# Tasks in the attention loops of layers 2 and 3: columns beside the scores, norms and rotary turns in single steps, key pieces traced behind the slot products

## The chip, the cores and the metric

The kernel runs on one core of a Trainium2 chip. A core has a matrix engine (TensorE, PE in profiles; its weight loads are shown apart as PEld), a vector engine (DVE), a scalar engine (ACT), a general engine (POOL) and a queue engine (SP) that issues most transfers. Each engine takes its instructions in one fixed order and waits where one isn't ready. The metric is the time of one execution on the device in microseconds (us); the median over several runs counts.

## The reference, cut to what matters

A model of four layers; each adds a cross attention to the tokens x (16 batches of 112 tokens, 256 wide, 1792 tokens in all) and then a feed-forward part. The change lies in the attentions of layers 2 and 3 and in what follows them:

```python
# layer 2 attention: 16 heads of 16, keys and values from a context of 375 rows
q = (query @ Wq.T + bq).reshape(B, Sq, H, Dh)
q = q * cq + _rotate_half(q) * sq_          # keys are turned likewise
scores = jnp.einsum('bqhd,bkhd->bhqk', q, k) * scale
probs = jax.nn.softmax(scores, axis=-1)
ctx = jnp.einsum('bhqk,bkhd->bqhd', probs, v).reshape(B, Sq, H * Dh)
return ctx @ Wo.T + bo
# layer 2 feed-forward: norm, 8 experts, the best 2 of each token
xn = x * jax.lax.rsqrt(jnp.mean(x * x, axis=-1, keepdims=True) + eps) * ln_w
logits = xn @ Wg + bg
vals, idx = jax.lax.top_k(logits, K)
...
# the stack
x = x + jnp.tanh(g_xattn[2]) * _L2_xattn_ref(_layernorm(x, axis=-1), ctx_1024, ...)
x = x + jnp.tanh(g_ffn[2]) * _L2_ffn_ref(_layernorm(x, axis=-1), ...)
```

Layer 3 is the same in kind: no rotary turn, a mask on the scores, 9 experts.

## The kernel before

**The attention loop** (`attention16`) serves layers 2 and 3. Its unit is four heads of one batch, 64 units in all, and step s of 70 begins unit s and carries earlier ones on. In order, TensorE does in step s:

- `scores(s)`: queries against keys, four heads into the four banks of one PSUM tile `sc` (tag sS, one buffer), columns 0 to 374 of each bank. In the first six steps idle matmuls (`spins`) follow into columns 376 to 503 of the same banks. DVE then takes each row's least score: in layer 2 by one reduction over all four banks (line 854), in layer 3 by four passes, one a bank (line 858).
- the tasks of the table `between[s]` (below);
- `by_keys`, `values`, `by_keys`: scores once more with the keys on the partitions (tile `st`, three banks, tag sT, one buffer), exponentials on ACT out of it, and weights times values into the tile `mi`;
- transposes in `mi` (`by_queries`, `maxima`, `by_rows`), with small DVE and ACT work after each.

Then DVE does the tasks of `behind[s]`, and SP gets the loads of keys and values for a later batch. Scores, tasks and transposes are pinned: `keep_in_program_order` puts an instruction behind everything traced before it on its engine. What is not pinned is ordered by a planner, which takes at each point the earliest traced of what it holds to be ready. The program's own dependency tracking adds the waits between engines.

**Tasks** are work that lies beside the attention. Early in the loop: statistics of late token tiles (`moments_at`, `roots_at`), their scaled rows (`scaled_at`), transposes of those rows into `hT` (`rows_at`: PE, then an ACT copy), and the query groups 2 and 3 of layer 2 (1 to 3 of layer 3), four batches each. Later in the loop, from `Outcome.tasks`: for each pair of token tiles the output projection and its addition to x (`add`), the norm of the result in nine small pieces in `behind`, the transposes of the rows, and the router's logits (`route`). A task's PSUM space is `three()`, a tile of tag sT, which is the one buffer that `by_keys` uses too (a2bt and a3bt in the profile; st is a2st and a3st).

**Layer 2's queries** are turned (`rotary`, lines 595 to 602): four DVE instructions on 448 columns for each half of a group, eight in one go, and then eight stores into slots (`to_slots`).

**After layer 2's loop** (`Outcome.rest`, `chosen`, `softmax_of`, `dispatch`): the last pair of tiles is finished, the best two experts of each token are found on DVE, two matmuls count them (`cp`, `tp`), more DVE work follows, and 56 matmuls (`slot`, line 1112) give the slots of the tokens, which the gather of the experts' rows needs (`tok`). Into this chain `fill(n)` traces pieces of the keys and values of layer 3 for ten batches (40 pieces; k3b in the profile): 4, 4 and 8 in `rest`, 8 at the start of `dispatch`, the other 16 ahead of the slot matmuls. Layer 3 has no such pieces, and its chain has idle matmuls (`spin`) instead.

Of the kernel before, what the change touches and what calls it, by code (L numbers as in the profile page):

```python
# [86 lines left out]
def flamingo_kernel(ctx, tc, a, out):  # L87
# [159 lines left out]
    def norm_rows(n, bank, tr=None, act=True, scale_by=None, keep=None, h=None):  # L247

        pin = tc.keep_in_program_order if tr else free
        if h is None:  # L250
            h = scaled(n, pin, keep)
        tp = bank(f"tp{n}")
        for c in range(2):
            (tr or nc.tensor.transpose)(tp[:, c * P:(c + 1) * P], h[:, c * P:(c + 1) * P], ident)
        if scale_by is not None:
            for c in range(2):
                nc.scalar.activation(
                    hT[:, c, n * P:(n + 1) * P], tp[:, c * P:(c + 1) * P], AF.Identity,
                    scale=col(scale_by, c),
                )  # L260
            return
        dst, src = hT[:, :, n * P:(n + 1) * P], tp[:, :D].rearrange("p (c t) -> p c t", c=2)
        pin(nc.scalar.copy(dst, src) if act else nc.vector.tensor_copy(dst, src))
# [330 lines left out]

    def rotary(pool, tag, dst, src, cos, sin, sign, fixed=False):

        rot = pool.tile(list(src.shape), F32, tag="rot", name=f"rot{tag}", bufs=1)
        pin = tc.keep_in_program_order if fixed else lambda i: i
        pin(nc.vector.stream_shuffle(rot, src, half_on))
        pin(nc.vector.scalar_tensor_tensor(rot, rot, sign, sin, ALU.mult, ALU.mult))  # L600
        pin(nc.vector.scalar_tensor_tensor(dst, src, sign, cos, ALU.mult, ALU.mult))
        pin(nc.vector.tensor_tensor(dst, dst, rot, ALU.add))

# [102 lines left out]

    def query_group(pool, tag, qT, wq, q_out, G, ps=None, mm=None):
# [33 lines left out]
    class Outcome:  # L741
# [30 lines left out]
        def tasks(self, between, behind, bias):  # L772


            for n, at, slots in zip(
                    range(0, NT - 2, 2), (18, 27, 36, 45, 54, 63),
                    ((29, 30, 32), (38, 39, 41), (47, 48, 50), (56, 57, 59), (65, 66, 68),
                     (67, 68, 69))):
                between.setdefault(at, []).append(
                    lambda three, mm, tr, n=n: self.add(n, three(), mm, pinned))  # L780
                todo = [bias[n // 2], moments_at(n, 1), moments_at(n + 1, 1)]
                todo += [lambda n=n, i=i: self.part(n, i, pinned) for i in range(4)]
                todo += [lambda n=n + i: self.scale(n, pinned) for i in range(2)]
                for i, t in enumerate(todo):

                    s = at + 1 + i if at < 63 else 64 + i // 3
                    behind.setdefault(s, []).append(t)
# [11 lines left out]
        def rest(self, tag, bias):  # L799
            n = NT - 2  # L800
            self.add(n, ps_pair(f"{tag}ops"))
            bias[n // 2]()
            fill(4)
# [5 lines left out]
            fill(4)  # L809
            self.route(n, ps_o(f"{tag}r"))  # L810
            fill(8)

    def attention16(pool, pp, tag, qT, kTs, vs_, store, nm=None, maskT=None, tasks=({}, {}), spins=(0, 0)):
# [202 lines left out]
    def dispatch(pool, keep, tag, one, two, gates, n_e):  # L1016
# [9 lines left out]
        sel2 = sel.rearrange("p e n -> p (e n)")  # L1026
        fill(8)
        what = small([P, 2, 2 * NT], "what")
# [75 lines left out]
        for k in range(2):  # L1104
# [3 lines left out]
            )  # L1108
        fill(len(filler))
        ps = ps_mm(f"{tag}slot")  # L1110
        for i in range(2 * NT):
# [3 lines left out]
            )  # L1115
        spin(ps_o(f"{tag}spin2")[:, :P], 14, at_lo[:, 0, :])

# [405 lines left out]
    with tc.tile_pool(name="l1x", bufs=2) as pool, tc.tile_pool(  # L1523
# [22 lines left out]
        def key_rotations(pool):  # L1546
# [14 lines left out]
            def turn(b, c):  # L1561
                k = held[b, c]
                rotary(pool, f"k{b}_{c}", k, k, tabs[:, 0, :], tabs[:, 1, :], 1.0, True)
                nc.gpsimd.dma_start(kr_store[b, :, c, :], k)
# [80 lines left out]
    def q_out2(qc, ps, G):  # L1645
        for c in range(2):
# [4 lines left out]
            con[:, at:at + S].unsqueeze(1).to_broadcast([P, 4, S]) for at in (C_COS, C_SIN)  # L1651
        )
        for c in range(2):
            four = qc[:, c, :].rearrange("p (b t) -> p b t", b=4)
            rotary(q_at, f"q{G}_{c}", four, four, cos, sin, -1.0)

# [189 lines left out]
    with tc.tile_pool(name="l3x", bufs=2) as pool:  # L1846
# [16 lines left out]
        def group3(G):  # L1863
            return lambda three, mm, tr: queries3(G, three(), mm)

# [208 lines left out]
```

## Time and profile before

| | us |
|---|---|
| median of 3 runs | 3017.82 (3011.21 to 3028.72) |
| the profiled execution | 3033.68 |
| its span, first to last instruction | 3031.8 |
| layer 2's loop, from the first scores to the last projection | 1440.85 to 1758.7 |
| from there to the first expert matmul of layer 2 | 1758.7 to 1864.0 |
| layer 3's loop | 2297.09 to 2658.0 |
| from there to the first expert matmul of layer 3 | 2658.0 to 2702.3 |

The profile is one execution. Lines of its page and answers name the engine, the line of the code, the operation and the tiles as out<-in. In lists in order of time the first two numbers are start and length in us, and a bracket gives the idle time before the instruction and what ended it. In lists of waits the numbers are us in total, times, and the longest. In tables of stretches each engine's busy time is followed by its count of instructions, and the last three numbers are the granted clock of TensorE as a share of full speed, the share of busy transfers, and GB/s.

### The profile page before, as it was taken

To read this page: it belongs to the slowest core of one execution; us is meant where nothing else is said; L and a number is where in the kernel's file an instruction comes from. 1 tells how busy PE (TensorE), PEld (TensorE's weight loads), DVE (VectorE), ACT (ScalarE), POOL (GpSimd) and SP (SyncE) were. 2 spreads that over 40 slices of the span, in tenths; PEclk is the share of its full clock that TensorE was granted. 3 is DMA by queue.
4 is the path that set the end of the run, shared out by engine and by line. 5 is a ranking of instruction groups with operands and counts; after the bars stand their busy time and mean duration, and the time that the engine had idled before them with its cause. 6 is when DMAs were issued, how large, how long until landed. Compare 5 with 4: busy or idle time off the path is not lost. (4 is left out here: it accounts for less than half of the span.)

```text
span 3031.8 us, 50238 instructions
## 1 busy us (share of the span) xinstructions
PE 2811.4 (93%) x19789; PEld 1985.1 (65%) x19789; DVE 1579.5 (52%) x4642; ACT 1040.5 (34%) x2392; POOL 249.5 (8%) x260
## 2 busy tenths in 40 slices
PE   6998999999999999998798878999998899889997
PEld 4666876566666666655565556888885555567775
DVE  5677874466666666666556632232224565542221
ACT  3556973244444444522234422111112333301111
POOL 1000000100000000000000001222210000012321
PEclk9999999999999999999789979999999999989999
DMA  4011334412112111010122146565532222135553
GB/s 166 27 32 59 108 118 157 165 56 65 58 54 65 61 32 34 25 39 12 40 68 84 53 136 236 150 181 176 165 96 79 71 73 68 38 114 153 157 153 96
DMA packets 118866, 281.99 MB, mean 93 GB/s; under 512 B 26904, under 2 KB 86664, under 8 KB 109712
## 3 DMA queue, kind: packets, MB, share of 16 engines
q1 hardware_dynamic: 95920, 242.50, 23.9%
q0 software_dynamic: 19040, 31.83, 5.1%
q10 hardware_dynamic: 3664, 4.37, 0.5%
q8 instruction: 160, 2.62, 0.4%
q14 instruction: 82, 0.67, 0.1%
HBM read 214.92 MB, written 81.35 MB: 98 GB/s over the span
## 5 line engine op out<-in xcount | busy, mean ns | idle before, releaser
L272 PE MATMUL b3ab<-b3xT,w 128*128 128x256 f32 (+1 forms) x864 | 196.1, 385 | 0.5 <-DVE b3xT L1167 0.5
L272 PEld LDWEIGHTS b3ab<-b3xT,w 128*128 128x128 f32 (+1 forms) x864 | 155.0, 183 | 39.4 <-issue 11.6
L1183 ACT ACTIVATE b2gs<-b2ab,bias 128x256 f32<-128x256 f32 x144 | 68.2, 474 | 321.0 <-PE b2ab L272 280.2
L394 PE MATMUL a1vps<-w_l1v,a1cb 128*125 128x512 f32 x360 | 172.1, 602 | 0.9
L1184 DVE SCALAR_TENSOR_TENSOR b2hid<-b2ab,bias,b2gs 128x256 f32<-128x256 f32 x144 | 69.6, 483 | 194.9 <-ACT b2gs L1183 194.9
L394 PE MATMUL a1kps<-a1cb,w_l1k 128*128 128x375 f32 x480 | 165.2, 486 | 0.0
L486 ACT ACTIVATE a1pe<-a1pe,a1mx 112x375 f32<-112x375 f32 x256 | 153.3, 603 | 0.0
L272 PE MATMUL b2ab<-b2xT,wa 128*128 128x256 f32 x576 | 150.3, 384 | 0.6 <-DVE b2xT L1169 0.6
L272 PE MATMUL b2ab<-b2xT,wb 128*128 128x256 f32 x576 | 149.0, 381 | 0.0
L476 DVE CUSTOM_DVE_ANT_0 a1pe<-a1sc,nm 112x375 f32<-112x375 f32 x256 | 126.0, 544 | 43.9 <-PE a1sc L394 43.9
L397 PEld LDWEIGHTS a1tp<-ident,a1pe 112*125 112x125 f32 x768 | 98.4, 188 | 58.2 <-issue 41.3
L1189 DVE TENSOR_TENSOR b3hid<-b3ab,b3gs 128x256 f32<-128x256 f32 x108 | 45.7, 423 | 172.7 <-ACT b3gs L1188 172.7
L1194 PE MATMUL b2yo<-wc,b2hid 128*128 128x256 f32 x576 | 132.1, 382 | 2.9 <-DVE b2y L1199 0.6
L858 DVE CUSTOM_DVE_ANT_0 a3ms<-a3sc,first_cb 112x375 f32<-112x375 f32 x256 | 124.5, 543 | 17.3 <-PE a3sc L835 16.8
L1188 ACT ACTIVATE b3gs<-b3ab 128x256 f32<-128x256 f32 x108 | 41.3, 382 | 260.1 <-PE b3ab L272 233.5
L885 ACT ACTIVATE a3pT<-a3st 125x1008 f32<-125x1008 f32 x86 | 86.3, 1004 | 128.4 <-PE a3st L835 128.4
L1194 PEld LDWEIGHTS b2yo<-wc,b2hid 128*128 128x128 f32 x576 | 108.0, 190 | 21.3 <-DVE b2y L1199 7.0
L272 PEld LDWEIGHTS b2ab<-b2xT,wa 128*128 128x128 f32 x576 | 110.5, 192 | 16.4 <-DVE b2xT L1169 1.2
L272 PEld LDWEIGHTS b2ab<-b2xT,wb 128*128 128x128 f32 x576 | 110.6, 192 | 15.4
L854 DVE TENSOR_REDUCE a2mx<-a2sc 112x4 f32<-112x1500 f32 x64 | 109.6, 1713 | 18.4 <-PE a2sc L835 18.1
L394 PEld LDWEIGHTS a1kps<-a1cb,w_l1k 128*128 128x128 f32 x480 | 85.8, 190 | 49.1 <-DVE a1pT L400 3.3
L885 ACT ACTIVATE a2pT<-a2st 125x1008 f32<-125x1008 f32 x86 | 86.3, 1004 | 81.9 <-PE a2st L835 81.9
(481 smaller groups left out, 5648.9 us busy)
## 6 DMA issues: line engine op xcount, KB each, us to landing
w<-all_w SPq DMA_DIRECT2D x36, 704.0 KB
wa<-in_w_l2e1a SPq DMA_DIRECT2D x18, 1024.0 KB
wb<-in_w_l2e1b SPq DMA_DIRECT2D x18, 1024.0 KB
wc<-in_w_l2e SPq DMA_DIRECT2D x18, 1024.0 KB
all_w<-in_w SPq DMA_DIRECT2D x24, 704.0 KB
a2vs<-k2v SPq DMA_DIRECT2D x16, 750.0 KB
a2v<-a2vs SPq DMA_DIRECT2D x16, 750.0 KB
a3v<-a3vs SPq DMA_DIRECT2D x16, 750.0 KB
```

Source lines behind the costliest of these rows:

```text
L272: (mm or nc.tensor.matmul)(dst, lhs(k), rhs(k), start=(k == 0), stop=(k == 1))
L394: pin(nc.tensor.matmul(*args, **kw))
L397: pin(nc.tensor.transpose(*args))
L476: pin(nc.vector.tensor_tensor_reduce(pe[:, 2 * p + j, :], sc[:S, j, :KV], made["nm"], 1.0, FMAX, ALU.add, ALU.min, mx[:, j:j + 1],))
L486: pin(nc.scalar.activation(e, sc[:S, j, :KV] if mask_of is None else e, AF.Exp, bias=mx[:, j:j + 1], scale=1.0 if mask_of is None else -1. ...
L854: pinned(nc.vector.tensor_reduce(mx[:, :, 16], sc[:S, :, :KV], AX.X, ALU.min))
L858: pinned(nc.vector.tensor_tensor_reduce(ms, sc[:S, j, :KV], nm, 1.0, FMAX, ALU.add, ALU.min, mx[:, j, 16:17]))
L885: nc.scalar.activation(pT[:, :n, :], st[:KC, :n, :3 * S], AF.Exp)
L1183: nc.scalar.activation(s[:fn], pa, AF.Silu, bias=bias(0, f))
L1184: nc.vector.scalar_tensor_tensor(hid[:fn, f, :], pb, bias(1, f), s[:fn], ALU.add, ALU.mult)
L1189: nc.vector.tensor_tensor(hid[:fn, f, :], pb, s[:fn], ALU.mult)
L1194: nc.tensor.matmul(po[:, i * D:(i + 1) * D], hid[:fn, f, i * P:(i + 1) * P], w2[:fn, f, :], start=(f == 0), stop=(f == nf - 1),)
```

## The change

- `room()` takes the place of `three()` for rows, additions and routes: it returns columns 376 to 503 of the four banks of the step's own score tile (from step 64, where no scores are left, a new tile of the same tag). The addition's matmuls are cut from 256 to 128 columns for it, 16 for 8. Query groups keep `three()`. Rows of layer 3 go on being taken in pairs, those of layer 2 singly.
- In layer 2 the early tasks move: statistics one tile a step in steps 0 to 5, roots in quarters, rows in steps 9 to 14, query groups in steps 14 and 17 instead of 5 and 8. `rotary` becomes a list of parts; for groups 2 and 3 each part and the stores are tasks of their own in `behind`, steps 14 to 21 and 22 to 29.
- In both layers the additions stand 8 steps apart (23 to 63) instead of 9 (18 to 63); rows follow after 10 and 11 steps, routes after 13.
- All `fill` calls in `rest` and at the start of `dispatch` go. In layer 2 all 40 key pieces are traced behind the slot matmuls, in place of the 14 idle ones there.

```diff
+        if len(tp.shape) == 2:
+            tp = tp[:, :D].rearrange("p (c t) -> p c t", c=2)
         for c in range(2):
-            (tr or nc.tensor.transpose)(tp[:, c * P:(c + 1) * P], h[:, c * P:(c + 1) * P], ident)
+            (tr or nc.tensor.transpose)(tp[:, c, :], h[:, c * P:(c + 1) * P], ident)
...
-        q_out(qc, ps, G)
-        to_slots(qT[:, :, G * GT:(G + 1) * GT], qc, nc.sync if mm else nc.scalar)
+        todo = list(q_out(qc, ps, G) or ())
+        todo.append(lambda: to_slots(
+            qT[:, :, G * GT:(G + 1) * GT], qc, nc.sync if mm else nc.scalar))
+        if later is None:
+            for t in todo:
+                t()
+        else:
+            later += todo
...
     def rows_at(n, m=2, scale_by=None):
-        def task(three, mm, tr):
-            ps = three()
+        def task(room, three, mm, tr):
+            ps = room()
             for i in range(m):
-                norm_rows(n + i, lambda _: ps[:, i, :], tr, scale_by=scale_by, h=hs.pop(n + i))
+                norm_rows(n + i, lambda _: ps[:, 2 * i:2 * i + 2, :], tr, scale_by=scale_by,
+                          h=hs.pop(n + i))
...
         def add(self, n, ps, mm=None, pin=free):
             for i in range(2):
-                mm2(ps[:, i, :D], lambda k: hT[:, k, (n + i) * P:(n + i + 1) * P],
-                    lambda k: self.wo[:, k, :], mm)
-            xs = x[:, n:n + 2, :]
-            pin(nc.vector.scalar_tensor_tensor(xs, ps[:, :2, :D], self.g, xs, ALU.mult, ALU.add))
+                for c in range(2):
+                    mm2(ps[:, 2 * i + c, :], lambda k: hT[:, k, (n + i) * P:(n + i + 1) * P],
+                        lambda k: self.wo[:, k, c * P:(c + 1) * P], mm)
+            xs = x[:, n:n + 2, :].rearrange("p i (c d) -> p (i c) d", c=2)
+            pin(nc.vector.scalar_tensor_tensor(xs, ps, self.g, xs, ALU.mult, ALU.add))
...
-            for n, at, slots in zip(
-                    range(0, NT - 2, 2), (18, 27, 36, 45, 54, 63),
-                    ((29, 30, 32), (38, 39, 41), (47, 48, 50), (56, 57, 59), (65, 66, 68),
-                     (67, 68, 69))):
+            for n, at in zip(range(0, NT - 2, 2), (23, 31, 39, 47, 55, 63)):
+                last = at == 63
...
                 for i in range(2):
-                    between.setdefault(slots[i], []).append(rows_at(n + i, 1, self.scale_by))
-                between.setdefault(slots[2], []).append(
-                    lambda three, mm, tr, n=n: self.route(n, three()[:, 0, :], mm, pinned))
+                    between.setdefault(at + (4 if last else 10) + i, []).append(
+                        rows_at(n + i, 1, self.scale_by))
+                between.setdefault(at + (6 if last else 13), []).append(
+                    lambda room, three, mm, tr, n=n: self.route(n, room()[:, 2, :], mm, pinned))
...
-            sc = pp.tile([P, 4, 512], F32, tag="sS", name=f"{tag}sc{u}", bufs=1)
+            sc = tiles["sc"] = pp.tile([P, 4, 512], F32, tag="sS", name=f"{tag}sc{u}", bufs=1)
...
-            for i, t in enumerate(between.get(s, ())):
-                t(lambda: pp.tile([P, 3, 512], F32, tag="sT", name=f"{tag}bt{s}_{i}", bufs=1), mm, tr)
+            def room():
+
+                if s >= units:
+                    tiles["sc"] = pp.tile([P, 4, 512], F32, tag="sS", name=f"{tag}sp{s}", bufs=1)
+                return tiles["sc"][:, :, KV + 1:KV + 1 + P]
+
+            for t in between.get(s, ()):
+                t(room, lambda: pp.tile([P, 3, 512], F32, tag="sT", name=f"{tag}bt{s}", bufs=1), mm, tr)
...
-        fill(len(filler))
         ps = ps_mm(f"{tag}slot")
...
-        spin(ps_o(f"{tag}spin2")[:, :P], 14, at_lo[:, 0, :])
+
+        if filler:
+            fill(len(filler))
+        else:
+            spin(ps_o(f"{tag}spin2")[:, :P], 14, at_lo[:, 0, :])
...
+        turns = {2: [], 3: []}
+
         def group2(G):
-            return lambda three, mm, tr: queries2(G, three(), mm)
+            return lambda room, three, mm, tr: queries2(G, three(), mm, turns[G])
+
+        def later_tiles():
+
+            at = {s: [moments_at(8 + s, 1)] for s in range(6)}
+            for first, n, m in ((4, 8, 4), (8, 12, 2)):
+                parts = root_parts(n, m, pinned)
+                for i in range(4):
+                    at.setdefault(first + i, []).append(parts[i])
+            for n in range(8, 14):
+                at.setdefault(min(n, 12), []).append(
+                    lambda n=n: hs.update({n: scaled(n, pinned)}))
+
+            for G, first in ((2, 14), (3, 22)):
+                for i in range(9):
+                    at.setdefault(first + min(i, 7), []).append(lambda G=G: turns[G].pop(0)())
+            return at
...
-                tasks=outcome2.tasks({
-                    0: [moments_at(8, 4)], 2: [rows_at(8)], 3: [rows_at(10), moments_at(12, 2)],
-                    5: [group2(2)], 6: [rows_at(12)], 8: [group2(3)],
-                }, {
-                    0: [roots_at(8, 4)], 1: [scaled_at(8)], 2: [scaled_at(10)],
-                    4: [roots_at(12, 2)], 5: [scaled_at(12)],
-                }, prepare),
+                tasks=outcome2.tasks(
+                    {9: [rows_at(8, 1)], 10: [rows_at(9, 1)], 11: [rows_at(10, 1)],
+                     12: [rows_at(11, 1)], 13: [rows_at(12, 1)], 14: [group2(2), rows_at(13, 1)],
+                     17: [group2(3)]},
+                    later_tiles(), prepare),
                 spins=(6, 0),
```

More of the change, by code (lines that the diff above doesn't have):

```diff
@@ L257, in norm_rows @@
                 nc.scalar.activation(
-                    hT[:, c, n * P:(n + 1) * P], tp[:, c * P:(c + 1) * P], AF.Identity,
+                    hT[:, c, n * P:(n + 1) * P], tp[:, c, :], AF.Identity,
                     scale=col(scale_by, c),
@@ L261, in norm_rows @@
             return
-        dst, src = hT[:, :, n * P:(n + 1) * P], tp[:, :D].rearrange("p (c t) -> p c t", c=2)
+        dst, src = hT[:, :, n * P:(n + 1) * P], tp
         pin(nc.scalar.copy(dst, src) if act else nc.vector.tensor_copy(dst, src))
@@ L593, in flamingo_kernel, with rotary_parts, shuffle @@
     half_on = [(r // 16) * 16 + (r + 8) % 16 for r in range(32)]
[L595 to L602, printed above, removed]
+    def rotary_parts(pool, tag, dst, src, cos, sin, sign, pin=free):
+        rot = []
+        def shuffle():
+            rot.append(pool.tile(list(src.shape), F32, tag="rot", name=f"rot{tag}", bufs=1))
+            pin(nc.vector.stream_shuffle(rot[0], src, half_on))
+        return [
+            shuffle,
+            lambda: pin(nc.vector.scalar_tensor_tensor(
+                rot[0], rot[0], sign, sin, ALU.mult, ALU.mult)),
+            lambda: pin(nc.vector.scalar_tensor_tensor(dst, src, sign, cos, ALU.mult, ALU.mult)),
+            lambda: pin(nc.vector.tensor_tensor(dst, dst, rot[0], ALU.add)),
+        ]
     def kv_store(tag):
@@ L705, in first_keys, with query_group @@
             load_k(kTs, store, b)
-    def query_group(pool, tag, qT, wq, q_out, G, ps=None, mm=None):
+    def query_group(pool, tag, qT, wq, q_out, G, ps=None, mm=None, later=None):
         qc = pool.tile([P, 2, GT], F32, tag="qc", name=f"{tag}qc{G}", bufs=2)
@@ L772, in tasks @@
         def tasks(self, between, behind, bias):
-            for n, at, slots in zip(
-                    range(0, NT - 2, 2), (18, 27, 36, 45, 54, 63),
-                    ((29, 30, 32), (38, 39, 41), (47, 48, 50), (56, 57, 59), (65, 66, 68),
-                     (67, 68, 69))):
+            for n, at in zip(range(0, NT - 2, 2), (23, 31, 39, 47, 55, 63)):
+                last = at == 63
                 between.setdefault(at, []).append(
-                    lambda three, mm, tr, n=n: self.add(n, three(), mm, pinned))
+                    lambda room, three, mm, tr, n=n: self.add(n, room(), mm, pinned))
                 todo = [bias[n // 2], moments_at(n, 1), moments_at(n + 1, 1)]
@@ L784, in tasks @@
                 for i, t in enumerate(todo):
-                    s = at + 1 + i if at < 63 else 64 + i // 3
-                    behind.setdefault(s, []).append(t)
+                    behind.setdefault(64 + i // 3 if last else at + 1 + i, []).append(t)
                 for i in range(2):
-                    between.setdefault(slots[i], []).append(rows_at(n + i, 1, self.scale_by))
-                between.setdefault(slots[2], []).append(
-                    lambda three, mm, tr, n=n: self.route(n, three()[:, 0, :], mm, pinned))
+                    between.setdefault(at + (4 if last else 10) + i, []).append(
+                        rows_at(n + i, 1, self.scale_by))
+                between.setdefault(at + (6 if last else 13), []).append(
+                    lambda room, three, mm, tr, n=n: self.route(n, room()[:, 2, :], mm, pinned))
             return between, behind
@@ L800, in rest @@
             n = NT - 2
-            self.add(n, ps_pair(f"{tag}ops"))
+            ps = ps_pair(f"{tag}ops").rearrange("p i (j d) -> p (i j) d", d=P)[:, 2:6, :]
+            self.add(n, ps)
             bias[n // 2]()
-            fill(4)
             moments(n, 2)
@@ L808, in rest @@
                 norm_rows(i, ps_pt, scale_by=self.scale_by, h=hs.pop(i))
-            fill(4)
             self.route(n, ps_o(f"{tag}r"))
-            fill(8)
     def attention16(pool, pp, tag, qT, kTs, vs_, store, nm=None, maskT=None, tasks=({}, {}), spins=(0, 0)):
@@ L1026, in dispatch @@
         sel2 = sel.rearrange("p e n -> p (e n)")
-        fill(8)
         what = small([P, 2, 2 * NT], "what")
@@ L1562, in turn @@
                 k = held[b, c]
-                rotary(pool, f"k{b}_{c}", k, k, tabs[:, 0, :], tabs[:, 1, :], 1.0, True)
+                for part in rotary_parts(
+                        pool, f"k{b}_{c}", k, k, tabs[:, 0, :], tabs[:, 1, :], 1.0, pinned):
+                    part()
                 nc.gpsimd.dma_start(kr_store[b, :, c, :], k)
@@ L1652, in q_out2 @@
         )
+        parts = []
         for c in range(2):
             four = qc[:, c, :].rearrange("p (b t) -> p b t", b=4)
-            rotary(q_at, f"q{G}_{c}", four, four, cos, sin, -1.0)
+            parts += rotary_parts(
+                q_at, f"q{G}_{c}", four, four, cos, sin, -1.0, pinned if G > 1 else free
+            )
+        return parts
     def queries2(G, *args):
@@ L1863, in group3 @@
         def group3(G):
-            return lambda three, mm, tr: queries3(G, three(), mm)
+            return lambda room, three, mm, tr: queries3(G, three(), mm)
         spin(ps_pair("spin3")[:, 0, :], 12)
```

## The prediction

> **What bounds the kernel now.** I read the page's engine row first, then the waits of TensorE in the attention loops of layer 2 (1440.85 to 1758.7 us) and layer 3 (2297.09 to 2658.0), then busy time by stretch, then single steps in order of time (a step runs from the start of its scores to that of the next; the lengths below are such differences).
>
> ```profile
> span 3031.8 us, 50238 instructions
> PE 2811.4 (93%) x19789; PEld 1985.1 (65%) x19789; DVE 1579.5 (52%) x4642; ACT 1040.5 (34%) x2392; POOL 249.5 (8%) x260
> ```
>
> TensorE (PE) is busy in 93% of the span, so only its idle time and its clock can be won. The waits that end idle time of PE in the loop of layer 2, and one row of layer 3's:
>
> ```profile
> PE a2mi L838 <- DVE a2qa L866: 14.4, 30, 1.7
> PE a2st L835 <- ACT a2pT L885: 8.5, 19, 0.8
> PE a2sc L835 <- DVE a2mx L854: 5.4, 2, 3.6
> PE a2bt L838 <- DVE h L242: 3.1, 1, 3.1
> PE a2st L835 <- DVE both L767: 1.7, 4, 0.5
> ...
> PE a3st L835 <- DVE both L767: 2.0, 4, 0.7
> ```
>
> The columns are total us, times, longest. A task holds the key-side scores (st) up for 1.7 us in all of layer 2's loop, 2.0 in layer 3's (with 2.8 more there behind other readers: hT 0.9, x 0.8, h 1.1). The change's first part has very little to win. The two rows with 3.6 and 3.1 are single bursts on VectorE (DVE) in steps 0 to 8. Those steps also cost clock:
>
> ```profile
> 1440.85:1507.68 66.83, 52.29 (x469) 34.13 (x470) 35.70 (x89) 16.11 (x26) 0.00 (x0) 0.77 0.14 38
> 1507.68:1552.09 44.41, 41.28 (x528) 27.12 (x527) 22.05 (x38) 14.71 (x26) 0.00 (x0) 0.65 0.26 66
> 1552.09:1733.14 181.05, 161.41 (x2723) 107.04 (x2722) 124.88 (x283) 81.67 (x144) 0.00 (x0) 1.00 0.24 71
> ...
> 2512.25:2519.08 6.83, 5.99 (x93) 4.28 (x95) 3.87 (x19) 2.42 (x4) 0.00 (x0) 1.00 0.38 125
> 2519.08:2525.91 6.83, 6.54 (x79) 4.21 (x71) 3.03 (x16) 1.26 (x2) 0.00 (x0) 0.50 0.10 24
> ```
>
> Length and busy PE come first, the granted clock is third from the end: 0.77 and 0.65 in steps 0 to 17 of layer 2, 1.00 in steps 18 to 63.
>
> **Part 1, the columns beside the scores.** A task's matmuls now write columns 376 to 503 of the score tile, behind scores(s) and ahead of all else of step s on PE. The reduction of scores(s) on DVE was traced earlier and reads the same tile. Does a write to other columns wait for it?
>
> ```profile
> 1441.78 1.60 PE L835 MATMUL a2sc<-rows,ident 128*128 128x128 f32 x12
> 1443.42 1.72 DVE L854 TENSOR_REDUCE a2mx<-a2sc 112x4 f32<-112x1500 f32 x1 [2.02 <-PE a2sc L835]
> ...
> 1632.91 0.90 PE L835 MATMUL a2sc<-a2kT,a2qT 32*112 32x375 f32 x8
> 1633.81 0.44 PE L838 MATMUL a2bt<-ident,h 128*128 128x128 f32 x2
> 1634.23 1.72 DVE L854 TENSOR_REDUCE a2mx<-a2sc 112x4 f32<-112x1500 f32 x1
> ...
> 1644.34 0.28 DVE L866 TENSOR_TENSOR a2qa<-a2mi,a2qT 128x112 f32<-128x112 f32 x1 [1.29 <-PE a2mi L838]
> 1644.67 0.32 PE L838 MATMUL a2mi<-ident,a2o 112*128 112x112 f32 x1 [0.44 <-DVE a2qa L866]
> ```
>
> The first pair is step 0: the idle spin matmuls write exactly those columns, and the reduction, which does not read them, starts when the last has ended. The last pair is the reverse order in tile mi: PE writes columns of its own and still waits for DVE to have read others (30 such waits in the table). So a task waits until the reduction ends. Step 38, in the middle, gives the price: scores end at 1633.81, where the row task starts today, and the reduction at 1634.23 + 1.72 = 1635.95. The wait is 2.1 us; an unhurried step (45) has 1.9. I take 2.05. PE keeps its order, so values, by_keys and the transposes of the step all stand behind it, and exp on ScalarE and qa on DVE behind those: nothing covers it. The waits inside a step that remain (0.44 for qa, 0.41 for exp) lie later in it and don't shrink.
>
> In layer 3 the reduction is four passes. Step 32: scores 2472.97 + 0.90 = 2473.87, the fourth pass closes at 2476.12, so 2.25 us; I take 2.2. Here a rule weighs in: the Trainium skill, PSUM — Partial Sum Buffer, "PSUM bank collisions raise a hardware error", says to guard "by **bank × quadrant** (by bank is the simple version), not by address". By bank, a row task of layer 3 would wait for two passes only, a route for three, an addition at first for one (0.93, 0.47 and 1.4 us less; 8, 4 and 6 of them: 17.7 us less). But in tile a3bt the transpose into bank 1 waits 0.46 us for ScalarE reading bank 0 (the wait PE a3bt <- ACT hT, five times), so the row says the whole tile, and I take that.
>
> Count of tasks in steps that have scores: layer 2, rows in steps 9 to 13 (in step 14 the row stands behind a 3 us query group, free), then 6 additions, 8 rows, 4 routes; layer 3, 5 row pairs and the same 18. The addition's 16 matmuls of 128 columns take the time of 8 of 256: 28 matmuls of 128 take 3.29 us (0.117 each, 1.9 us), against 1.99 now. Nothing there.
> - Layer 2, steps 18 to 63: 18 x 2.05 = +36.9, less the 1.7 above: **+35.2**.
> - Layer 3: 23 x 2.2 = +50.6, less 2.0 + 2.8: **+45.8**.
> The tail (steps 64 to 69) has no reduction: nothing.
>
> **Part 2, norms and turns by steps (layer 2, steps 0 to 17).** Today 111.2 us, 61.4 of them at half clock. New: steps 0 to 3 like today's step 0 (scores 0.90, spins 1.60, reduction 1.72 and hand-overs: 4.35), 17.4; step 4 5.6 as measured; step 5 4.7 (today's step 4 less one by_keys); twelve steps without tasks as at full clock today (steps 60 to 62: 10.9; 33 to 35: 10.8), 43.4; two query groups at 3.8 (step 9 of layer 3, 7.24 against 3.46); six rows 1.8; five waits of 2.1, 10.5. Sum 91.0: **-20.2**. The 16 DVE instructions of the turns (0.62 to 0.65 each) and the norms go one or a few to a step, where DVE has 0.5 us or more free; in odd steps of 2.98 us they may push the reduction by 0.2, five times. The 8 query stores of each group go into SP's queue in steps 21 and 29 instead of 5 and 8, some 10 us of issuing (8 key loads take 10.33) ahead of the next key load, which has about six steps; the queries are wanted in steps 32 and 48. Hidden.
>
> **Part 3, key pieces behind the slot products.**
>
> ```profile
> 1787.84 0.40 DVE L1025 CAST d2sel<-two 128x112 bf16<-128x112 f32 x1
> ...
> 1810.91 0.21 PE L1038 MATMUL d2cp<-d2sel,tri_b 128*128 128x112 bf16 x1
> ...
> 1861.18 0.48 PE L1159 MATMUL b2xt<-ident,b2xb 128*128 128x128 f32 x1 [3.70 <-DMA b2xb<-s2rows,d2tok]
> ```
>
> The routing chain waits 22.7 us (1788.2 to 1810.9) behind 24 pieces; then the gather stands bare, 3.7 + 0.9 us. Traced later, the pieces lose their precedence, but the planner may still put them into gaps. Yet they have their own pace: all ten batches are still needed, 8 us each by the stores of values (k3bv copies at 1797.9, 1806.3, 1813.9, 1821.8), 80 us from 1771.3, when their weights land. So layer 2's experts start some 4.6 us earlier from the covered gather and 3 or so from waits filled: **-8**. The 3.3 us of spins lay in the gather wait and are worth nothing. Bounds: if no piece fits into the chain, 1758.7 + 38 (layer 3's chain without pieces, 2658.0 to 2696.0) + 80 = 1877 against 1864: +13; if expert work fills every store wait (12.8), -20. The expert weights then queue on SP among the pieces' loads and stores, which speaks against the good end.
>
> **Clock.** The skill, TensorE: Matmul & The Clock Gate, "What's actually happening", lets the clock fall after an idle window of about 3.4 us; by it waits of 2.2 us cost no clock. The rows differ: at 2519.08 the gate fell for 6.83 us after a stretch with PE 88% busy and no gap above 0.84 us. One such stretch costs 2.7 us (steps 41 and 42 of layer 3: 6.37 and 5.20 against 4.75 and 4.09 at full clock; 4.75 is 3.46 without a task and 1.29 for the route, as in layer 2). More idle time should bring more: I take three more, **+8** (bounds 0 and 40).
>
> **Sum:** 35.2 + 45.8 - 20.2 - 8 + 8 = +60.8. The profiled execution took 3033.7 us (span 3031.8 and 1.9 around it), 15.9 above the median; I put the difference on the median: 3017.8 + 61 = **3079 us**.
>
> **Rivals.** (a) *Columns are free*, the other sign: the task's write waits for nothing. Then parts 1 and 2 give -1.7 - 4.8 - 30.7, part 3 -8: 2973 us. It decides at the wait per task: 45.2 us of gains over 46 tasks, so below 1.0 us each the kernel gets faster, provided the clock stays as it is. For it: the columns are disjoint; against it: the pairs above. (b) *Clock*: the waits in steps 9 to 13 hold layer 2 at half clock as today (+15) and nine more stretches fall (+24): 3110 to 3125. For it: the loop of layer 3 falls already; against: steps 0 and 1 of layer 3 idle 2 us of 5 and fell for 3.4 us only. (c) *Pieces late*: +13 in place of -8: 3100. (d) Waits half as long, because DVE reaches the reduction sooner than now: 3010 to 3035.
>
> **Chances.** Likeliest 0.60, (a) 0.10, (b) 0.14, (c) 0.11, (d) 0.05. A difference within 0.5% (15 us) can't be told from none by this kernel's runs, which spread by 17.5. Faster 0.11 (a and a little of d), same 0.04, slower 0.85. The likeliest's own range is 3050 to 3105; the 8 in 10 range leaves out (a), most of (d) and the top of (b): 3028 to 3124.
>
> **What would show it.** Right: a new row of waits PE a2sc (and a3sc) <- DVE a2mx (a3ms, a3mx), some 23 times each near 2 us; both loops' task steps longer, steps 0 to 8 of layer 2 shorter with no long burst of turns; d2cp soon after d2sel; no bare gather before b2xt. Wrong: task matmuls that start with the reduction running; a clock below 0.9 in steps 18 to 63; b2ab starting after 1864 in the chain's own count.

## The result, and the profile after

The changed kernel takes 3244.7 us (median of 4 runs, 3235.0 to 3251.1) against 3023.3 before: ratio 1.0732, 95% interval 1.0678 to 1.0786. That is slower, as forecast, but by 221 us where 61 were forecast. The profiled execution took 3235.0 us, the shortest of the four; beside the profiled 3033.7 of before it is 201.4 longer.

The page's head for the kernel after: TensorE (PE) is busy for 115 us *longer* than before (2811.4), for nearly the same matmuls.

```profile
span 3233.2 us, 50395 instructions
PE 2926.8 (91%) x19873; PEld 2063.1 (64%) x19873; DVE 1579.3 (49%) x4642; ACT 1042.7 (32%) x2392; POOL 250.1 (8%) x260
```

The waits of PE (us in total, times, longest), kernel after. The first four rows hold the new waits (before had 5.4 and 2.1 us of those in the third and fourth); the fifth was there before:

```profile
PE a3sc L851 <- DVE a3mx L871: 31.0, 13, 2.8
PE a2sc L851 <- DVE a2mx L867: 27.5, 13, 2.5
PE a2sc L848 <- DVE a2mx L867: 26.4, 16, 2.2
PE a3sc L848 <- DVE a3mx L871: 24.9, 11, 2.3
...
PE a2mi L851 <- DVE a2qa L879: 14.0, 30, 0.9
...
PE a3sc L851 <- ACT hT L265: 2.4, 5, 0.5
```

They are the waits that the prediction described: a task's matmul into the score tile stands until the reduction (a2mx, a3mx) has read it. Together 109.8 us, of which 8.5 are not the tasks' (6.5 and 2.0 remain where no task writes there, in the first run below): 101.3 for 46 tasks, 2.2 each, against 98.0 forecast (36.9 + 10.5 + 50.6). The last row shows that the tile counts as a whole in layer 3 too: the second row of a pair waits in one bank for a reader of another.

The same in order of time, step 23, which carries an addition (start, length; in brackets the wait and what ended it):

```profile
1567.38 0.90 PE L848 MATMUL a2sc<-a2kT,a2qT 32*112 32x375 f32 x8
1568.68 1.71 DVE L867 TENSOR_REDUCE a2mx<-a2sc 112x4 f32<-112x1500 f32 x1
1570.44 3.50 PE L848 MATMUL a2sc<-w_l2o,hT 128*128 128x128 f32 x16 [2.16 <-DVE a2mx L867]
```

The wait of 2.16 is the one forecast. The 3.50 us behind it are not: 16 such matmuls were put at 1.9. The records show half clock from 1570.77 to 1574.18. The table of stretches tells how common that is (length, busy PE, ..., granted clock third from the end): steps 0 to 8 of layer 2, 9 to 14, 15 to 17, 18 to 63 (up to the start of step 63, as in the prediction), and steps 18 to 63 of layer 3; the last line is the same stretch of layer 3 in the kernel before:

```profile
1441.95:1482.47 40.52, 33.56 (x442) 23.89 (x442) 23.48 (x53) 11.60 (x16) 0.00 (x0) 0.92 0.13 42
1482.47:1534.44 51.97, 40.39 (x372) 24.07 (x372) 17.55 (x42) 13.60 (x26) 0.00 (x0) 0.57 0.12 36
1534.44:1548.70 14.26, 12.69 (x185) 7.62 (x184) 8.18 (x15) 5.45 (x12) 0.00 (x0) 1.00 0.22 68
1548.70:1818.65 269.95, 219.29 (x2762) 149.09 (x2762) 132.90 (x296) 82.75 (x144) 0.00 (x0) 0.72 0.17 51
...
2523.97:2829.36 305.39, 251.12 (x2942) 164.04 (x2941) 137.23 (x595) 80.39 (x136) 0.00 (x0) 0.77 0.14 46
```
```profile
2406.61:2629.98 223.37, 203.70 (x2903) 132.47 (x2902) 135.64 (x598) 79.66 (x136) 0.00 (x0) 0.95 0.20 63
```

Steps 18 to 63 of layer 2 ran at 1.00 before and run at 0.72 now: 181.05 us have become 269.95. Of these 89 us, 31 are added idle time (the waits, less small gaps that slower work fills) and 58 added busy time, 219.29 against 161.41: the same matmuls are slower. In layer 3 the stretch grew from 223.37 to 305.39 us, and its clock fell from 0.95 to 0.77.

By stage (profiled executions, the one of before as in its table): layer 2's loop 317.9 to 404.0 (+86.1), from there to the first expert matmul 105.3 to 99.6 (-5.7), experts 433.0 to 440.9 (+7.9), layer 3's loop 360.9 to 473.1 (+112.1), the rest +1.0.

### The profile page after: what moved, and what is told of

It reads as the page before. It is cut to its first block, busy times and chain, and to the rows that moved or that the text cites. A ratio compares the mean times of both kernels' runs of the same rounds, so it can differ in the third digit from the quotient of the medians.

```text
span 3233.2 us, 50395 instructions
## 1 busy us (share of the span) xinstructions
PE 2926.8 (91%) x19873; PEld 2063.1 (64%) x19873; DVE 1579.3 (49%) x4642; ACT 1042.7 (32%) x2392; POOL 250.1 (8%) x260
## 5 line engine op out<-in xcount | busy, mean ns | idle before, releaser
L399 PEld LDWEIGHTS a1tp<-ident,a1pe 112*125 112x125 f32 x768 | 98.4, 188 | 58.3 <-issue 41.4
L867 DVE TENSOR_REDUCE a2mx<-a2sc 112x4 f32<-112x1500 f32 x64 | 109.9, 1717 | 20.4 <-PE a2sc L848 20.2
```

Source lines behind the costliest of these rows:

```text
L399: pin(nc.tensor.transpose(*args))
L867: pinned(nc.vector.tensor_reduce(mx[:, :, 16], sc[:S, :, :KV], AX.X, ALU.min))
```

## The experiments

Theory A: the waits are as forecast, and the clock that falls because of them is the missing part. Rivals: the new tables and smaller matmuls lower the clock (B), or writing beside the scores costs in itself (C). All ratios are to the kernel before, run beside each kernel.

### A tile of its own, and the tasks later in their step

```diff
-            def room():
...
-            for t in between.get(s, ()):
-                t(room, lambda: pp.tile([P, 3, 512], F32, tag="sT", name=f"{tag}bt{s}", bufs=1), mm, tr)
+            for i, t in enumerate(between.get(s, ())):
+                three = lambda: pp.tile([P, 3, 512], F32, tag="sT", name=f"{tag}bt{s}_{i}", bufs=1)
+                t(lambda: three()[:, 0, :].rearrange("p (j d) -> p j d", d=P), three, mm, tr)
```

> The changed kernel with one thing undone: a task writes into a tile of the tag sT again (its four blocks of 128 columns in one bank), not into the columns beside the scores. The tables of steps, the single-step turns, the 16 matmuls of 128 columns and the pieces behind the slot products stay. Theory A (each task's wait for the reduction, and a TensorE clock that falls after such waits, are the whole loss): the waits on a2mx and a3mx go, the clock in steps 18 to 63 of layer 2 is back above 0.97 and in layer 3 near 0.95; parts 2 and 3 remain with -20 and about 0, so 3023 - 20 = 3003 us (2985 to 3020). Rival B (the clock falls because of the new tables, the turns between other work or the smaller matmuls; the columns cost only the wait itself, some 110 us less 6): 3245 - 104 = about 3140, with a clock still near 0.92.

Measured: 3037.2 us, 1.0059 (1.0022 to 1.0097). B's 3140 is out, and so is A's 3003: the columns are nearly the whole loss, but the parts that were to gain 20 or so gain nothing here. A also expected a clock above 0.97 in steps 18 to 63 of layer 2; in the profiled execution, one of the longer ones (3050.7 us), it was 0.88, and what lowers it there no run shows.

In the next run the columns stay, and the loop over the tasks moves from behind `scores(s)`:

```diff
             if (s, 1) in rounds:
                 by_keys(rounds[s, 1])
+            for t in between.get(s, ()):
+                t(room, lambda: pp.tile([P, 3, 512], F32, tag="sT", name=f"{tag}bt{s}", bufs=1), mm, tr)
             if 4 <= s < units + 4:
                 by_queries(s - 4)
```

> The changed kernel, columns beside the scores included, with the tasks moved within their step: behind values and the second key-side scores, just ahead of the transposes. By then the reduction is over. Theory A: no wait for a2mx or a3mx worth the name; in their place the next scores wait for the reader of the task's columns (a ScalarE copy of 0.5 to 0.6 us or the addition on VectorE), less the transposes that lie between: 0 to 0.4 us for each of 46 tasks. Clock as before the change. 3003 + 0 to 20: about 3012 us (2990 to 3035). Rival B: 3140 as for the tile of its own. Rival C (writing beside scores costs in itself, whatever the order): near 3245.

Measured: 3046.3 us, 1.0104 (1.0073 to 1.0136); steps 0 to 17 of layer 2 took 84.0 us at full clock. It is more than A's range (2990 to 3035), but near the tile of its own and far from 3245, so C is out: the columns themselves cost little once the reduction has ended.

### Idle matmuls in the waits

```diff
+            if s < units and between.get(s):
+                sp = pp.tile([P, 3, 512], F32, tag="sT", name=f"{tag}idle{s}", bufs=1)
+                spin(sp[:, 0, :P], 7, None, mm)
             for t in between.get(s, ()):
```

> The changed kernel with seven idle matmuls (128 columns, into a tile of tag sT, 0.27 us each at full clock by the spins of step 0, so 1.9 us) traced between the scores and each step's tasks. They lie inside the wait: TensorE computes nothing more, and a task still cannot start before the reduction has ended. Theory A: the waits stay, as idle matmuls and a rest of 0.1 to 0.4 us, but the clock no longer falls: 0.95 or more over the span, and the time is that of the tile of its own plus the waits, 3003 + 100 = about 3103 us (3080 to 3130). If the clock falls because TensorE is loaded or for any reason but idle time, the clock stays near 0.91 and the time is 3245 or more. If the long half-clock stretches come from one or two other places, something between, 3170 to 3220.

Measured: 3110.8 us, 1.0303 (1.0247 to 1.0360), clock 0.973 in the profiled execution. Work that computes nothing was added, and the changed kernel became some 130 us (4%) faster. Steps 18 to 63 of both layers in this run, and what is left of the waits:

```profile
1543.17:1765.42 222.25, 196.66 (x3001) 139.77 (x3000) 131.43 (x296) 81.89 (x144) 0.00 (x0) 0.98 0.21 62
2456.14:2709.94 253.80, 225.79 (x3181) 156.92 (x3180) 136.09 (x595) 79.73 (x136) 0.00 (x0) 1.00 0.17 56
```
```profile
PE a3sc L851 <- DVE a3mx L871: 9.0, 13, 1.0
PE a2sc L848 <- DVE a2mx L867: 8.1, 15, 1.8
PE a3sc L848 <- DVE a3mx L871: 7.3, 11, 2.0
PE a2sc L851 <- DVE a2mx L867: 7.3, 13, 0.8
```

Without the 8.5 us that are not the tasks', 0.5 us of each wait is left. The tasks still start behind the reduction, but PE is seldom idle meanwhile, and the clock stays at 0.98 and 1.00 where it was 0.72 and 0.77. This tells the two costs of one wait apart: its own length, and what it does to the clock of the work behind it.

How long must a wait be? Three idle matmuls in place of seven leave some 1.2 us of each:

```diff
-                spin(sp[:, 0, :P], 7, None, mm)
+                spin(sp[:, 0, :P], 3, None, mm)
```

> The changed kernel with three idle matmuls (0.8 us) instead of seven in each task's wait, so that some 1.3 us of each wait stay idle. Waits, covered ones included, are as in the changed kernel, so only the clock differs. If the clock falls by the length of single gaps and 1.3 us is too short for it: as with seven, 3111 us at 0.97. If any idle time counts in proportion: about 1.3 / 2.2 of the way from 3111 to 3245, so 3190 at 0.94. Theory A takes a middle: 3140 us (3115 to 3180), clock 0.95 to 0.965.

Measured: 3172.0 us, 1.0517 (1.0483 to 1.0552), clock 0.944. No threshold shows between these lengths: with 0.5, 1.2 and 2.2 us of idle time a task the ratios are 1.030, 1.052 and 1.073, the clocks 0.973, 0.944 and 0.914. A's range for the time holds it, its range for the clock (0.95 to 0.965) does not. The rival in proportion comes nearest: it put the time at 3190, or at some 3167 with the waits as they are (an estimate, from 0.5, 1.2 and 2.2 us). The next run shortens the real waits instead:

```diff
             if 4 <= s < units + 4:
                 values(s - 4)
+            for t in between.get(s, ()):
+                t(room, lambda: pp.tile([P, 3, 512], F32, tag="sT", name=f"{tag}bt{s}", bufs=1), mm, tr)
             if (s, 1) in rounds:
```

> The changed kernel with the tasks traced behind values (12 matmuls, some 0.9 us, with by_keys ahead of them in one step of three) instead of directly behind the scores. The wait that is left is about 1.2 us in two tasks of three and 0 to 0.3 in the third: 46 x 0.8 = 37 us in sum instead of 105. Theory A without any loss of clock: 3040 + 30 = 3070 us. With the clock falling in proportion to idle time: 37 / 105 of 134 us more, 3115. A fall that needs gaps of 2 us: 3070 at a clock of 0.965 or more.

Measured: 3119.0 us, 1.0319 (1.0283 to 1.0354). Steps 18 to 63 of both layers, and the waits:

```profile
1538.72:1758.86 220.14, 187.91 (x2762) 127.36 (x2762) 132.38 (x296) 82.42 (x144) 0.00 (x0) 0.85 0.22 62
2464.67:2725.32 260.65, 229.09 (x2942) 148.61 (x2941) 137.14 (x595) 80.19 (x136) 0.00 (x0) 0.84 0.18 54
```
```profile
PE a3sc L851 <- DVE a3mx L871: 17.1, 11, 2.1
PE a2sc L848 <- DVE a2mx L867: 16.8, 16, 1.8
PE a3sc L848 <- DVE a3mx L871: 12.2, 11, 2.0
PE a2sc L851 <- DVE a2mx L867: 10.4, 9, 1.7
```

56.5 us of waits instead of 109.8, and the clock still falls to 0.85 and 0.84. The value in proportion (3115 expected) held here too, though the tasks' own waits are 48 us where 37 were expected.

### Tasks ahead of the scores

```diff
+            for t in between.get(s, ()):
...
+                    read += t(room, three, mm, tr) or []
...
             if s < units:
...
+                scores(s, sc)
+            for r in read:
+                r()
```

A task here issues its matmuls and returns what reads them (ScalarE's copies, VectorE's additions), which follows the scores.

> The changed kernel with the same columns beside the scores, but a task's matmuls are traced ahead of the scores of its step, into the new score tile, and what reads them (ScalarE's copy, VectorE's addition) behind the scores. TensorE has then nothing to wait for that it did not wait for anyway: the scores need the same tile free. Theory A (order in one tile is the whole harm of the columns): no waits on a2mx and a3mx from tasks, clock 0.96 or more, time like that of the tile of its own or a little less: 3030 us (3010 to 3050). If the columns cost in themselves: over 3100.

Measured: 3046.3 us, 1.0081 (1.0053 to 1.0108). In steps 2 and 3 of layer 3 the idle matmuls that follow the scores overwrite the transposed rows of tiles 4 to 7 before they are copied, so those queries are not the model's; what is issued is unchanged. No wait for the reduction is left but 6.2 us of the start; the rows wait 17.3 us in sum for their scaled input (h) instead. Order in the tile decides, not place in it.

### The spacing, the steps and the pieces

In the changed kernel, the pieces go back (and the four `fill` calls ahead of them):

```diff
+        fill(len(filler))
         ps = ps_mm(f"{tag}slot")
...
-        if filler:
-            fill(len(filler))
-        else:
-            spin(ps_o(f"{tag}spin2")[:, :P], 14, at_lo[:, 0, :])
+        spin(ps_o(f"{tag}spin2")[:, :P], 14, at_lo[:, 0, :])
```

> The changed kernel with part 3 alone undone: the key pieces of layer 3 go back into the chain behind layer 2's loop (4, 4, 8, 8 and the rest ahead of the slot matmuls). By the balance of the two profiles part 3 gave 5.8 us up to the first expert matmul and then lost 7.9 up to layer 3's loop. Theory A: part 3 is worth about nothing, so 3245 - 2 us (3232 to 3258). Rival (the pieces behind the slot products push the experts and their bias work late, and the 7.9 are theirs alone, while the 5.8 come from the shorter last tasks): 8 to 15 us faster than the changed kernel, 3230 to 3237.

Measured: 3230.9 us, 1.0696 (1.0642 to 1.0749); against 1.0732 the intervals overlap, and neither side is shown. In the profile the way to the experts is 108.3 us (99.6 with the pieces late) and the experts 433.6 (440.9): the gain and the loss that cancel.

With the tile of its own as well as the pieces put back:

> Both part 1 and part 3 undone: tasks in a tile of tag sT, key pieces back in the chain; what is left of the change is part 2 (norms and turns by steps) and the new spacing of the additions. It measured 3037 against 3015 with the pieces behind the slot products. If part 3 is worth nothing (profiles: 5.5 gained before the experts, 8.2 lost behind them): 1.005 of before, about 3030 us. If part 3 itself costs some 10 to 14 us (the run with the pieces put back into the changed kernel was that much shorter, within its uncertainty): 1.001 or 1.002, 3018 to 3021, and part 2 is then worth nothing in time rather than the -20 forecast.

Measured: 3034.3 us, 1.0068 (1.0035 to 1.0101). Beside 1.0059 with late pieces, part 3 is worth nothing that can be measured. Now the additions, rows and routes also go back to their old steps:

```diff
-            for n, at in zip(range(0, NT - 2, 2), (23, 31, 39, 47, 55, 63)):
+            for n, at, slots in zip(
+                    range(0, NT - 2, 2), (18, 27, 36, 45, 54, 63),
...
-                    between.setdefault(at + (4 if last else 10) + i, []).append(
+                    between.setdefault(slots[i], []).append(
...
-                between.setdefault(at + (6 if last else 13), []).append(
+                between.setdefault(slots[2], []).append(
```

> Parts 1 and 3 undone as before, and the additions, rows and routes back at the steps that they had (18, 27 and so on, 9 apart); the norms and turns by steps stay, and so do the 16 matmuls of 128 columns. With the new spacing the same kernel measured 1.0068 of before, though its steps 0 to 8 were 26 us shorter than in the profile of before; its steps 48 to 63 were 9 us longer. If the spacing (tasks in heavier steps, and a clock that falls there) costs the most: 0.998 to 1.000, 3012 to 3018 us. If it's the turns and norms in steps 9 to 29: 1.006, 3034 us.

Measured: 3017.9 us, 0.9998 (0.9977 to 1.0019). The spacing costs 0.7% where the tasks have the tile sT: with it, an addition falls into steps 31 and 55, which run two key-side scores through that one tile, and PE idles 1.25 us in such a step (0.57 in step 54 with the old spacing). Layer 3's steps 18 to 63 go from 225.6 to 216.6 us. Whether the spacing costs as much in the changed kernel, where tasks don't use sT, was not tried.

That leaves norms and turns by steps at nothing in the medians, though the forecast gain stands in the trace. Is the baseline at fault? The kernel before was traced again, with no edit:

> The kernel before, unchanged, traced a second time: its profiled execution took 3033.7 us at a clock of 0.963, while most of its runs lie at 3008 to 3020 and 0.968 to 0.974. If the first profile caught a slow pass through layer 2's loop (61 of the first 111 us at half clock), the loop takes some 300 us here instead of 317.9 and its steps 0 to 17 some 92 to 96 instead of 111.2; the 20 us that part 2 was to gain were then never there in most runs. If the runs differ elsewhere, the loop stays at 315 to 320 and another stage is shorter.

Measured: 3015.3 us, 0.9985 (0.9953 to 1.0017), the profiled execution 3022.8. First its steps 0 to 17 of layer 2, then those of the run with the old spacing:

```profile
1441.05:1551.04 109.99, 93.65 (x995) 61.59 (x995) 57.74 (x126) 30.85 (x52) 0.00 (x0) 0.72 0.18 50
```
```profile
1443.48:1531.57 88.09, 71.33 (x995) 46.62 (x995) 48.89 (x110) 30.63 (x52) 0.00 (x0) 0.96 0.16 52
```

The expectation of a shorter loop is out: 110.0 us again, 88.1 with part 2. Yet the same code of these 18 steps took 93.1 in the run with idle matmuls at the end (below) and 100.8 in the one with the pinned mask, so before is not always as slow there (it took 111.2 once more in the one with late pieces alone). Some is given back: 2.8 us in steps 18 to 31 (58.3 against 55.5) and 3.1 between the loop and the experts. How the rest of 22 us disappears from the medians stays open; a trace shows one execution of each.

### What the late pieces collide with

The waits of the kernel after, behind the first expert matmul, and VectorE (DVE) in order of time there:

```profile
DVE bqs L1824 <- DMA a3vs<-k3bv: 10.4, 1, 10.4
...
PE b2ab L274 <- DVE b2hid L1205: 8.1, 1, 8.1
```
```profile
1952.21 0.48 DVE L1205 SCALAR_TENSOR_TENSOR b2hid<-b2ab,bias,b2gs 128x256 f32<-128x256 f32 x1 [0.54 <-ACT b2gs L1204]
...
1963.06 0.16 DVE L1824 TENSOR_TENSOR bqs<-cols 128x2 f32<-128x2 f32 x1 [10.37 <-DMA a3vs<-k3bv]
...
1964.04 0.48 DVE L1205 SCALAR_TENSOR_TENSOR b2hid<-b2ab,bias,b2gs 128x256 f32<-128x256 f32 x1
```

A sum of two columns for layer 3 (bqs, 0.16 us) waits for the last store of the pieces, whose memory its tile takes over. The expert's products b2hid stand behind it on DVE, and PE behind those. To test it, the kernel before with part 3 alone and the set-up of bqs and the mask traced later:

```diff
-                    0: [sums_begin], 3: [lambda: prepare.extend(prepare3())],
+                    0: [sums_begin], 12: [lambda: prepare.extend(prepare3())],
```

> The kernel before with part 3 alone (all key pieces behind the slot products), and with layer 3's mask and bias set up behind block 12 of the experts instead of block 3, so that VectorE does not stand before a bias sum (bqs) that waits for the pieces' last store. Theory A (the 8 us lost behind the first expert matmul are that wait, with the expert's products b2hid queued behind it): the loop's end to the first expert matmul 100 us instead of 105.3, from there to layer 3's loop 433 as before instead of 441; in sum 6 us less than before: 3011 us (3003 to 3018), ratio 0.998. If the 8 us come from the pieces' transfers or from the expert weights behind them, 441 stays, and the ratio is 1.001.

Measured: 3011.1 us, 0.9974 (0.9955 to 0.9992), but the edit did not do its work: the planner took bqs as early as before, and the wait is still there. So this is the kernel before with part 3 and no more. Its median is 7 us shorter than before's, but its trace shows no such gain where part 3 works: the way to the experts gained 5.1 us (105.3 to 100.2) and the experts lost 5.4 (433.0 to 438.4).

```profile
DVE bqs L1780 <- DMA a3vs<-k3bv: 10.3, 1, 10.3
...
PE b2ab L272 <- DVE b2hid L1183: 7.9, 1, 7.9
```

So both are pinned in VectorE's order:

```diff
-            nc.vector.tensor_tensor(bqs, cols[:, at:at + 2], cols[:, at + 2:at + 4], ALU.add)
+            pinned(nc.vector.tensor_tensor(bqs, cols[:, at:at + 2], cols[:, at + 2:at + 4], ALU.add))
-            nc.vector.tensor_copy(off, off.bitcast(I32))
+            pinned(nc.vector.tensor_copy(off, off.bitcast(I32)))
```

> The kernel before with part 3 alone, and layer 3's bias sum (bqs) and the first instruction of its mask now pinned on VectorE behind block 12 of the experts; traced later alone, the planner had taken them as early as before. Theory A (VectorE's order: the products b2hid of the first expert stand behind a bias sum that waits 10.3 us for the pieces' last store): the 8 us gap of TensorE 20 us behind the first expert matmul goes, from there to layer 3's loop 431 to 433 us instead of 438.4, the way from the loop's end to the experts stays at 100, and the ratio falls from 0.9974 to about 0.995 (3003 us). If another instruction takes the wait over, or the gap is the transfers' own: 438 stays, 0.9974.

Measured: the gap is gone, bqs runs at 2151.1, and from the first expert matmul to layer 3's loop it takes 429.5 us instead of 438.4 (before: 433.0), with 100.3 ahead of it. The cause of the 8 us is shown. The median, 3011.7 us or 0.9981 (0.9956 to 1.0006), cannot tell these 9 us from nothing.

### Idle matmuls at the end, and all of it together

The next edit is made to the kernel before with part 3 and the later, unpinned set-up:

```diff
+            if s >= units:
+                idle = pp.tile([P, 4, 512], F32, tag="sS", name=f"{tag}idle{s}", bufs=1)
+                spin(idle[:, 0, :P], 4, None, mm)
```

> The same as the run with the late pieces and the later mask, and in steps 64 to 69 of both loops four idle matmuls a step (0.27 us each, 6.5 us in a loop) into the score tile, which is free there. TensorE idles in these steps for up to 1.8 us at a time, and 24 us from the last of them on ran at half clock in each loop's end. Theory A: the idle matmuls stand partly in those gaps (some 5 us of them in all), the half-clock stretch at the end shrinks to 10 us or less: 5 to 12 us gained in both loops together, 3002 us (2990 to 3010), ratio 0.995. If the gaps are not what lowers the clock, or the idle matmuls lie where no gap is: 5 to 10 us longer than the run without them, ratio 1.0 or more.

Measured: 3008.9 us, 0.9964 (0.9945 to 0.9984). Beside 0.9974 without them that is no difference that counts, though the half-clock stretch at layer 2's end was 13.7 us instead of 27.3.

The last kernel is the changed one with the edits shown above for the tile of its own, the old steps, the pinned set-up and the idle matmuls at the end:

> The change with its costs taken out: tasks in a tile of tag sT at the steps that they had before, norms and turns by steps kept, key pieces behind the slot products, layer 3's bias and mask pinned behind block 12 and four idle matmuls a step in steps 64 to 69. From the single runs: 0.9998 with the norms and turns, -0.5% from the pieces if the pinned set-up works, -0.1% from the idle matmuls: 0.993 to 0.995, 2997 to 3003 us. If the parts disturb each other as in the run with a tile of its own (0.6% more with the changed spacing and late pieces): 1.0 or more.

Measured: 2997.2 us (2990.6 to 3003.7), 0.9920 (0.9896 to 0.9943): faster than both kernels. The parts of the change are worth 0.8% once the columns and the spacing are left out, bqs is pinned and the ends are filled. That is more than was expected (0.993 to 0.995) and more than the runs of the parts add up to (0.02% + 0.19% + 0.10%); no run explains the difference. Its page's head:

```profile
span 2995.1 us, 50589 instructions
PE 2780.0 (93%) x19969; PEld 1973.0 (66%) x19969; DVE 1575.7 (53%) x4642; ACT 1041.5 (35%) x2392; POOL 249.8 (8%) x260
```

## Why the prediction was wrong

- **Clock (+8, bounds 0 and 40): the step that failed.** The sum took it as "three more" half-clock stretches. Idle matmuls in the waits put it at 1.0732 - 1.0303 = 0.0429, or some 130 us, of which perhaps 9 are loss that before has too (an estimate: clock 0.974 in the median of that run and 0.970 in before's, at 22 us for 0.01). The mechanism was named, and rival (b) had its direction, but its size was taken from the isolated falls of layer 3's loop, 2.7 us each, as if a few more waits made a few more falls. The row to size it by stood in the prediction: steps 0 to 17 of before, with four waits of 1.7 to 3.6 us, ran at 0.77 and 0.65, and it was used only for what part 2 would gain and for steps 9 to 13 in rival (b). The loops with a wait of some 2 us in 17 of 45 steps now run at 0.72 and 0.77. Break-even of rival (a), "below 1.0 us each ... provided the clock stays as it is", fails with it: waits of 1.2 us already cost clock.
- **The rule** of the Trainium skill (TensorE: Matmul & The Clock Gate, "What's actually happening") would make the loss zero, since no wait here passes 2.8 us. Doubting it was right; the row that was put against it, a single fall of 6.83 us, was the wrong one for the size.
- **Part 1, right.** The task waits for the reduction of the whole tile, 101.3 us measured against 98.0. The price by bank (17.7 us less), which the row of tile a3bt spoke against, did not come up. 16 matmuls of 128 columns, "nothing there", took 3.50 us, most of it at half clock; at full clock, in the run with seven idle matmuls, they took 2.05, and the 8 of before 1.99.
- **Part 2 (-20): shown in one stage, not in the time.** In the changed kernel itself steps 0 to 17 took 106.7 us (91.0 forecast, 111.2 before), with a clock of 0.57 in steps 9 to 14, where five of the waits lie. With the tile of its own and the old spacing they are 22 us shorter in the traces (88.1); the medians give 0.9998 (0.9977 to 1.0019). The new spacing, counted as neutral, costs 0.7% in a tile of its own.
- **Part 3 (-8): not shown.** The medians differ: nothing with the tile of its own (1.0068 and 1.0059), 7 us alone in the kernel before (0.9974), which its trace does not show where part 3 works. In the changed kernel the chain gave 5.7 us: d2cp follows d2sel at once, and the gather is covered. But "experts start some 4.6 us earlier ... and 3 or so" looked at SP's queue and not at DVE's: layer 3's bias sum waits there for the pieces' last store, and the experts behind it lose 8.
- **The sum without clock** was 52.8; the run with idle matmuls in the waits has 92 (0.0303 x 3023), and 80 between the profiled executions. Of these 80, steps 18 to 63 of layer 2 have 41.2 (35.2 forecast), layer 3's loop 42.7 (45.8), steps 0 to 17 of layer 2 -11.0 (-20.2), the way to the experts and the experts 4.5 (-8), and the rest 2.6. So parts 2 and 3 are most of what is missing. The 12 between 80 and 92 no run places.

## What to carry to other kernels

A wait of 1 to 3 us on TensorE that returns in every second or third step of a loop is priced twice: its length, and the clock of what follows; look in the profile for a stretch that already has such waits, and take its granted clock for the new one. A task put beside another's data in one tile should stand where that data's reader is done, or ahead of its writer. When a transfer is moved later, look at every engine for small instructions that wait for it or for its memory, and at what stands behind them.

## What was not expected of the hardware

- The granted clock fell to half in slices of 3.41 us (a single one, 1570.77 to 1574.18, up to eleven, 1778.98 to 1816.53) in loops in which PE was busy 81 to 82% of the time and idle for at most 2.8 us at once.
- What came ahead of a fall was a slice with little work in it, but none without work. The two attention loops of the changed kernel have 133 slices of 3.41 us at full clock. In the 34 that a fall follows, PE was busy for 0.18 to 0.68 of the slice; of the other 99, only 3 are below 0.70. Half clock ended behind a slice in which PE was busy throughout in 31 of 32 cases. The lines show a slice without and one with a fall behind it (2.52 and 1.25 us busy of 3.41), and the longest stretch at half clock:

```profile
1563.94:1567.36 3.42, 2.52 (x54) 1.75 (x51) 1.75 (x2) 2.12 (x3) 0.00 (x0) 1.00 0.46 80
1567.36:1570.77 3.41, 1.25 (x12) 0.62 (x12) 2.58 (x5) 0.30 (x2) 0.00 (x0) 1.00 0.41 68
...
1778.98:1816.53 37.55, 32.51 (x334) 21.70 (x334) 13.62 (x35) 10.10 (x18) 0.00 (x0) 0.50 0.03 12
```

- This fits the loss by length of wait. A wait of 2.2 us that lies in one slice leaves 0.35 of it for work, one of 1.2 us 0.65, one of 0.5 us 0.85 (estimates, from 3.41 us), and with 0.5 us left of each wait only 5 of 207 slices were followed by a fall. It is a count and not a test, and it has exceptions: of the 10 falls in the loops of before, 4 followed slices with PE busy for 0.77 to 0.87.
- Clock explains the time between the changed kernel and the one with idle matmuls: in the profiled executions 0.059 between 0.914 and 0.973 goes with 121 us, some 21 us for each 0.01. It doesn't explain the rest of the loss, as that run is 92 us longer than before at the same clock or a higher one. The kernel before spreads by nearly the same measure: of 18 runs, those at 0.971 took 3009 to 3013 us and the one at 0.960 took 3037, some 24 us for 0.01.
